# A new order of chunks in the last two layers of a graph network, and a third buffer for gathered rows

## The chip, the cores and the metric

The kernel runs on one core of a Trainium2 chip. The metric is the time of one execution on the device in microseconds (us), as the median of several runs. Engines are named as in the profile: PE is TensorE, PEld its weight loads, DVE VectorE, ACT ScalarE, POOL GpSimd, SP SyncE. POOL issues the gathers (indirect DMAs), SP and ACT the plain DMAs.

## What is computed

Four layers on `x` of 4096 nodes by 256 features, all with the same weighted adjacency matrix `adj` (4096 by 4096, float32, mostly zeros; the first nodes have by far the most neighbours). After each layer the result is added to `x` and normalized by row.

```python
# layer 0: A @ (x * W)
# layer 1: two steps of R @ X and of top-p attention, each with its projections (R = A + I by row sums)
# layer 2
scores = inputs @ H_v
logits = where(adj != 0, adj * scores[None, :], -max)
weights = softmax over a row's neighbours
out = weights @ inputs
# layer 3
neighbor_node_features = adj @ node_features
neighbor_edge_features = einsum('ij,ji->i', adj, edge_features)[:, None]
out = concatenate((node_features, neighbor_node_features, neighbor_edge_features)) @ weight + bias
```

Layer 2 keeps two products of its output: `y3`, through the half of the layer-3 weight that belongs to neighbours, and `t3`, through the half that belongs to the node itself (with the node's own value added). Layer 3 then is `adj @ y3` plus `t3`, an edge term and the bias, and a row normalization.

## The kernel before

Nodes are cut into 32 blocks of 128 rows. A block's sum over neighbours is made in one of two ways:

- **hub blocks**, the first ones (`HUBS = (3, 6)`: three in layer 2, six in layer 3), multiply all 32 column blocks. A hub chunk is four of them: one panel of 256 KB loaded by SP (`loads`, six buffers), and four matmuls against rows that are in SBUF (`X2` in layer 2, `Y3` in layer 3).
- **list blocks**, all others, have a short list of columns found in layer 0 (`CAPS`, 4 to 7 slots of 128 entries). A list chunk is a piece of at most five slots: one packed block loaded by SP (`pc`, six buffers) and, per slot, one gather on POOL of 128 rows (`xg`, 24 buffers) and one matmul.

`product` (L1609) runs a layer: n=0 is layer 2 with rows from `x2d`, n=1 is layer 3 with rows from `y3d`. Layer 2 has 24 hub chunks and 35 list chunks (146 gathers), layer 3 has 48 and 29 (126 gathers). `evenly` (L1604) merges the two sequences by their relative position, so both last to the end. In this one sequence, `fetch` (L1616) issues loads and gathers for the chunk three places ahead (`FETCH = 3`), `weigh` (L1633) prepares the next chunk, and `multiply` (L1637) does the matmuls of the present one. In layer 2 `weigh` is `nbr_weights` (L1589): one ACT exponential per slot, one DVE product per chunk (L1593). Layer 3 has nothing to weigh. PE, ACT, DVE and POOL carry their work in the order that is written out; a queue that stands at a wait holds all behind it. SP is filled by a scheduler.

When a block's sum is complete, its end follows one chunk later: `out_2` (L1669) divides, normalizes on DVE, transposes and projects on PE (L463), and writes `y3d` (ACT queue, L1682) and `t3d` (SP queue, L1685). `out_3` (L1698) adds the bias, the edge term and `t3` (L1700 to L1702, the last reading the sum from PSUM), normalizes and writes the output. `before_3` (L1693) loads a block's `t3` back (`t3r`, seven buffers) with the block's first chunk. A sum in PSUM belongs to one bank: hub blocks use the bank A (`acc_tile("A")`), list blocks alternate between two others. Gathers of layer 3 (POOL) wait until all of `y3d` is written.

The change also touches the first attention step of layer 1, the "narrow" stage. There 32 blocks run through a pipeline whose pieces have planned times (`AT`, L1122). Per block, piece W (L1253) computes the index of five times 128 listed rows, pieces G0 to G4 (`fetch`, L1255) gather these rows on POOL into tiles `g_0`, `g_2` and `g_4` (two buffers each), piece PK (L1270) transposes part of them on PE, and piece PSA (L1313) multiplies them; this frees the tiles for the block after the next.

Of the kernel before, what the change touches and what calls it, by code (L numbers as in the profile page):

```python
# [11 lines left out]
F32 = mybir.dt.float32  # L12
# [6 lines left out]
P = 128  # L19
# [23 lines left out]
NB = 5  # L43
ORDER = (1, 3, 0, 2, 4)

TW = D + DA
# [3 lines left out]
NEW = 7  # L50
HUBS = (3, 6)
FETCH = 3
NM = 4
GUESS = (1.2, -0.129)
SLOPE, AIM, NEAR, MOVE, FEW = 0.07, 16, 32, 1.5, 70
# [12 lines left out]
LC = 512  # L68
# [5 lines left out]
def gnn_kernel(ctx: ExitStack, tc: tile.TileContext, x, pair, panels, W0, W1, W2T, W3T, U1T, U2T,  # L74
# [33 lines left out]
    def bank(shape, name, tag):  # L108
        if name in own_bank:
            tag = name  # L110
        return pools["psum"].tile(shape, F32, name=name, tag=tag, bufs=n_banks.get(tag, 1))
# [20 lines left out]
    for j in range(NT):  # L132
        t = big.tile([P, D + 1], F32, name=f"xw_{j}", tag=f"xa{j}", padded_shape=[P, D + 2])
# [80 lines left out]
    def acc_tile(which):  # L214
        return bank([P, 512], "acc", f"acc{which}")
# [175 lines left out]
    def gather(o, src, idx, c):  # L391
        nc.gpsimd.indirect_dma_start(out=o, out_offset=None, in_=src,  # L392
                                     in_offset=bass.IndirectOffsetOnAxis(ap=idx[:, c], axis=0))
# [160 lines left out]
    def find_0():  # L554
        for b in range(LE, NT):
            e = pools["e"].tile([P, N], F32, name="e")
            for h in range(NT // HB):
                t = e[:, h * HB * P:(h + 1) * HB * P]
                nc.sync.dma_start(t.rearrange("p (c x) -> p c x", x=JC * P),
                                  panels[b, h * HB // JC:(h + 1) * HB // JC].rearrange("c p k i -> p c (k i)"))  # L560
                yield
                nc.vector.tensor_reduce(seen[:, h * HB:(h + 1) * HB, b], t.rearrange("p (t i) -> p t i", i=P), AX.X,
                                        OP.max, apply_absolute_value=True)
# [54 lines left out]
    with tc.manual_schedule(engines=everything):  # L618
        sums_of_edges = edges_0()
        dense = (step for I in range(LE) for step in dense_0(I))  # L620
        find, lists, others = find_0(), list_columns(1, True), None
        left, active, n, heads = list(range(LE, NT)), [], 0, 3
# [17 lines left out]
        lists = others  # L640
# [250 lines left out]
    def cut(a):  # L891
# [3 lines left out]
        u, r = facts[n]["u"][:, I:I + 1], facts[n]["r"][:, I:I + 1]  # L895
        ties = small.tile([P, NM], F32, name="ties")
        nc.vector.tensor_scalar(rest, cand.rearrange("p a b -> p (a b)"), u, None, op0=OP.is_equal)
        nc.vector.tensor_reduce(ties, rest.rearrange("p (a b) -> p a b", a=NM), AX.X, OP.add)
        left = small.tile([P, NM], F32, name="left")
        nc.vector.tensor_tensor_scan(left, ones.to_broadcast([P, NM]), ties, r, op0=OP.mult, op1=OP.subtract)  # L900
        nc.vector.tensor_add(ties, ties, left)
# [3 lines left out]
        nc.vector.tensor_scalar(ties, ties, a["ud"], u, op0=OP.mult, op1=OP.add)  # L905
        m = N // NM
        for g in range(NM):
            eg = e[:, g * m:(g + 1) * m]
# [202 lines left out]
    for k in range(2):  # L1111
        t = const.tile([P, N // P + 1], BF16, name=f"ranks_{k}")
# [17 lines left out]
    def narrow(I):  # L1130


        sp, at_I, a = pools["sp"], slice(I, I + 1), {}
# [120 lines left out]

        def fetch(k):  # L1255
            if k % 2 == 0:
                a["pair", k] = sp.tile([P, 2 if k < NB - 1 else 1, TW], F32, name=f"g_{k}", bufs=2)
            to = a["pair", k - k % 2][:, k % 2, :]
            at_end = k % 2 == 0 and k < NB - 1
            gather(to, tab if at_end else tak, a["idx"], slice(k, k + 1))  # L1260
            a["g", k] = to[:, :D] if at_end else to[:, DA:]
# [109 lines left out]
    at = {}  # L1371
# [19 lines left out]
    def r_stream(blocks):  # L1391
        due, t = [], 0
        for b in blocks:
            if b == DENSE:
                run(lists)
            for _ in r_one(b, lambda f: due.append((t + LATE, f))):
                t += 1
                while due and due[0][0] <= t:
                    due.pop(0)[1]()
                yield  # L1400
        for _, f in due:
            f()

    everything = {getattr(mybir.EngineType, k) for k in ("PE", "Activation", "DVE", "Pool")}
    with tc.manual_schedule(engines=everything):
        r_blocks = list(range(LE, NT)) + list(range(DENSE, LE))
        side = r_stream(r_blocks)
# [37 lines left out]
    def r_dense():  # L1445

        stage = e_tile(2)
        xs = stage[:, :N // 2].rearrange("p (s k i) -> p s k i", s=2, k=JC)
        more = stage[:, N // 2:].rearrange("p (s b k i) -> p s b k i", s=2, b=2, k=JC)
        ps = [acc_tile("A"), acc_tile("R"), bank([P, 512], "acc2", "tp")]  # L1450
        given = {}

        def fetch(c):
            if c < NT // JC:
                pc = pools["gat"].tile([P, PIECE, P], F32, name="pc", bufs=N_PC[0])
                given[c] = [pc[:, :JC], more[:, c % 2, 0], more[:, c % 2, 1]]
                nc.sync.dma_start(xs[:, c % 2], qtab[c * JC * P:(c + 1) * JC * P, :].rearrange("(k p) d -> p k d", p=P))
                for b, t in enumerate(given[c]):
                    nc.sync.dma_start(t, panels[b, c])

        fetch(0)
        for c in range(NT // JC):
            fetch(c + 1)
            for k in range(JC):
                for b in range(DENSE):
                    nc.tensor.matmul(ps[b][:, :D], given[c][b][:, k, :], xs[:, c % 2, k], start=(c + k == 0),
                                     stop=(c * JC + k == NT - 1))
                yield
        for b in range(DENSE):
            new_t(b, ps[b], reload(qpd[b], 0))  # L1470

    none = iter(())
    with tc.manual_schedule(engines=everything):
        rest = r_dense()
# [122 lines left out]
    for I in range(NT):  # L1597
        t = big.tile([P, D + 2], F32, name=f"x2_{I}", tag=f"xa{I}")
# [2 lines left out]
    ends_in = ["x3", 4]  # L1601
    Y3 = [pools["x3"].tile([P, D], F32, name=f"y3_{I}") for I in range(NT)]

    def evenly(a, b):  # L1604

        turns = [((k + 0.5) / len(x), n, x[k]) for n, x in enumerate((a, b)) for k in range(len(x))]
        return [what for _, _, what in sorted(turns, key=lambda t: t[:2])]

    def product(n, src, width, inside, order, weights, end, first=None):  # L1609

        hubs = [(I, c, None) for I in range(HUBS[n]) for c in order]
        lists = [(I, m, ab) for I in range(NT - 1, HUBS[n] - 1, -1) for m, ab in enumerate(pieces(I))]
        chunks = evenly(hubs, lists)
        given, made, ps, going, at, had = {}, {}, {}, [], {}, {}

        def fetch(t):  # L1616
            I, m, ab = chunks[t]
            if first and I not in had:
                had[I] = first(I)
            if ab is None:  # L1620
                pc = pools["loads"].tile([P, JC, P], F32, name="panel", tag="panel")
                nc.sync.dma_start(pc, panels[I, m])
                given[t] = pc, inside[m * JC:(m + 1) * JC]
                return
            pc = pools["gat"].tile([P, PIECE, P], F32, name="pc", bufs=N_PC[0])
            nc.sync.dma_start(pc[:, :ab[1] - ab[0]], packed[I][m])
            xs = []
            for k in range(*ab):
                xs.append(pools["gat"].tile([P, src.shape[1]], F32, name="xg", padded_shape=[P, D + 2]))
                gather(xs[-1], src, idx_x, col(I, k))  # L1630
            given[t] = pc, xs

        def weigh(t):  # L1633
            pc, xs = given.pop(t)
            made[t] = (weights(pc, xs, len(xs)) if weights else pc), xs

        def multiply(t):  # L1637
            I, m, ab = chunks[t]
            if I not in ps:
                ps[I] = (bank([P, 2, LC], "acc", "lg")[:, 0, :] if ab and I % 2 else acc_tile("R" if ab else "A"))  # L1640
                at[I] = 0
            pc, xs = made.pop(t)
            n_all = NT if ab is None else CAPS[I]
            for k, xg in enumerate(xs):
                nc.tensor.matmul(ps[I][:, :width], pc[:, k, :], xg[:, :width], start=(at[I] == 0), stop=(at[I] == n_all - 1))  # L1645
                at[I] += 1
            if at[I] == n_all:
                going.append(end(I, ps[I], had.get(I)))

        with tc.manual_schedule(engines=everything):  # L1650
            for t in range(min(FETCH, len(chunks))):
                fetch(t)
            weigh(0)
            for t in range(len(chunks)):
                if t + FETCH < len(chunks):
                    fetch(t + FETCH)
                if t + 1 < len(chunks):
                    weigh(t + 1)
                before = list(going)
                multiply(t)  # L1660
                for g in before:
                    if next(g, g) is g:
                        going.remove(g)
            while going:
                for g in list(going):
                    if next(g, g) is g:
                        going.remove(g)
# [174 lines left out]
```

## Time and profile before

| | us |
|---|---|
| median of 3 runs (2638.25 to 2649.78) | 2639.12 |
| the profiled execution | 2997.28 |
| its span, first to last instruction | 2995.5 |
| layer 0 (first to last L549 matmul) | 4.4 to 482.6 |
| narrow stage (first to last L1313 matmul) | 585.8 to 1331.0 |
| layer 1, second step (L1086 matmuls) | 1430.2 to 2482.2 |
| layer 2 (list matmuls, L1645) | 2514.5 to 2756.9 |
| layer 3 (hub matmuls, L1645) | 2759.5 to 2983.3 |

| engine | busy us | share of the span |
|---|---|---|
| PE | 2275.7 | 76% |
| DVE | 2073.9 | 69% |
| POOL | 1694.0 | 57% |
| ACT | 1480.6 | 49% |

The profiled execution is one run with the profiler on, and is longer than the median run. A line of the timeline reads: start, length, engine, source line, operation, what it writes and reads, how many, and in brackets how long the engine had been idle before and what ended that. "remote" or "another core or an unknown queue" stands where nothing in the profile accounts for the end of a wait, "issue" where the engine waited for nothing that the profile shows. A float32 matmul leaves two records on PE.

### The profile page before, as it was taken

To read this page: it belongs to the slowest core of one execution; us is meant where nothing else is said; L and a number is where in the kernel's file an instruction comes from. 1 tells how busy PE (TensorE), PEld (TensorE's weight loads), DVE (VectorE), ACT (ScalarE), POOL (GpSimd) and SP (SyncE) were. 2 spreads that over 40 slices of the span, in tenths; PEclk is the share of its full clock that TensorE was granted. 3 is DMA by queue.
4 is the path that set the end of the run, shared out by engine and by line. 5 is a ranking of instruction groups with operands and counts; after the bars stand their busy time and mean duration, and the time that the engine had idled before them with its cause. 6 is when DMAs were issued, how large, how long until landed. Compare 5 with 4: busy or idle time off the path is not lost.

```text
span 2995.5 us, 37683 instructions
## 1 busy us (share of the span) xinstructions
PE 2275.7 (76%) x10680; PEld 1616.2 (54%) x10680; DVE 2073.9 (69%) x6152; ACT 1480.6 (49%) x2413; POOL 1694.0 (57%) x2778
## 2 busy tenths in 40 slices
PE   7887787677666776667988888888878864787587
PEld 5675564344333443435766666666656653555475
DVE  5785455765565665626578999999999991766366
ACT  0000112455454554545678888888899941343000
POOL 1007774444444444444358888888888754662663
PEclk9998898787777877778999999999999987899798
DMA  9978874333333333345531111111111115564574
GB/s 323 336 252 294 252 232 151 101 113 114 98 86 98 91 100 94 93 117 167 176 107 59 54 51 46 56 49 45 60 40 40 49 34 174 174 207 149 168 248 139
DMA packets 261978, 392.17 MB, mean 131 GB/s; under 512 B 41920, under 2 KB 170320, under 8 KB 260992
## 3 DMA queue, kind: packets, MB, share of 16 engines
q1 hardware_dynamic: 160992, 203.82, 21.5%
q0 software_dynamic: 46112, 131.50, 15.3%
q10 hardware_dynamic: 54656, 54.35, 5.3%
q8 instruction: 88, 1.44, 0.2%
q14 instruction: 130, 1.06, 0.1%
HBM read 329.25 MB, written 60.26 MB: 130 GB/s over the span
## 4 chain that ended last, share of the span: by engine, by line
DVE 18%; PE 17%; POOL 6%; issue 6%; ACT 6%; another core or an unknown queue 2%; DMA 0%; ACTq 0%; DVEq 0%; SPq 0%; POOLq 0%
PE acc L1645 5%; PE psa L236 4%; DVE cand L867 3%; PE acc L1086 2%; DVE e L913 2%; DVE tmp L861 2%; POOL xg L392 2%; PE lg L670 2%; DVE e L909 2%; ACT junk L780 2%; PE pt L225 1%; DVE top L844 1%; DVE rest L846 1%; PE po L463 1%
## 5 line engine op out<-in xcount | busy, mean ns | idle before, releaser
L236 PE MATMUL psa<-v,eT 128*128 128x256 f32 x2048 | 508.3, 395 | 74.9 <-ACT eT L227 68.0
L236 PEld LDWEIGHTS psa<-v,eT 128*128 128x128 f32 x2048 | 397.9, 198 | 153.4 <-ACT eT L227 87.4
L549 PE MATMUL acc<-xw,panel 128*128 128x257 f32 x1024 | 258.5, 403 | 35.0 <-DMA panel<-in_panels 22.4
L780 ACT ACTIVATE junk<-e,h 128x4096 bf16<-128x4096 f32 x64 | 237.5, 3711 | 47.3 <-POOL h L760 34.8
L549 PEld LDWEIGHTS acc<-xw,panel 128*128 128x128 f32 x1024 | 200.4, 202 | 92.7 <-issue 34.3
L392 POOL DMA_INDIRECT g<-tab,idx x64 | 63.1, 985 | 312.9 <-PE acc L1313 221.9
L225 PE MATMUL pt<-ident,e 128*128 128x128 f32 x1024 | 157.5, 284 | 101.4 <-DVE e L913 68.9
L786 ACT ACTIVATE junk<-e,h 128x4096 bf16<-128x4096 f32 x62 | 230.8, 3723 | 0.1
L247 ACT COPY xT<-ptx 128x256 f32<-128x256 f32 x96 | 35.7, 372 | 360.3 <-PE ptx L244 181.7
L463 PE MATMUL po<-u,xT 128*128 128x512 f32 x256 | 172.3, 810 | 51.0 <-ACT xT L247 26.2
L225 PEld LDWEIGHTS pt<-ident,e 128*128 128x128 f32 x1024 | 130.3, 147 | 145.4 <-issue 95.8
L867 DVE MAX8 cand<-tmp 128x8 f32<-128x128 f32 x1024 | 203.8, 281 | 1.1
L392 POOL DMA_INDIRECT xg<-qtab,idx_x x146 | 140.1, 959 | 93.6 <-issue 34.9
L227 ACT COPY eT<-pt 128x512 f32<-128x512 f32 x256 | 144.6, 588 | 91.3 <-PE pt L225 90.4
L392 POOL DMA_INDIRECT xg<-x2d,idx_x x146 | 144.3, 988 | 80.4 <-issue 38.7
L392 POOL DMA_INDIRECT pc<-in_pair,idx_a x146 | 149.2, 1022 | 66.3 <-issue 37.9
L392 POOL DMA_INDIRECT xg<-y3d,idx_x x126 | 120.9, 960 | 109.9 <-DMA t3d<-t 43.7
L1158 ACT ACTIVATE e<-lg 128x1024 f32<-128x1024 f32 x128 | 131.0, 1024 | 103.0 <-remote 58.5
L392 POOL DMA_INDIRECT xg<-ttab,idx_x x146 | 144.8, 992 | 60.5 <-issue 33.4
L1166 DVE MAX8 cand<-e 128x8 f32<-128x256 f32 x512 | 176.0, 412 | 3.2 <-ACT e L1158 3.2
L1155 PE MATMUL lg<-kT,qi 64*128 64x512 f32 x512 | 155.9, 684 | 2.9 <-DVE qp L515 2.5
L909 DVE SCALAR_TENSOR_TENSOR e<-e,ties 128x1024 f32<-128x1024 f32 x128 | 156.0, 1281 | 2.9
(347 smaller groups left out, 5674.3 us busy)
## 6 DMA issues: line engine op xcount, KB each, us to landing
panel<-in_panels SPq DMA_DIRECT2D x200, 256.0 KB
e<-in_panels SPq DMA_DIRECT2D x64, 512.0 KB
pc<-pk SPq DMA_DIRECT2D x53, 320.0 KB
e<-in_hubs ACTq DMA_DIRECT2D x6, 2048.0 KB
xg<-ttab SPq DMA_DIRECT2D x96, 128.0 KB
pc<-pk SPq DMA_DIRECT2D x39, 256.0 KB
pc<-in_panels SPq DMA_DIRECT2D x32, 256.0 KB
tab<-xi ACTq DMA_DIRECT2D x33, 160.0 KB
```

Source lines behind the costliest of these rows:

```text
L225: nc.tensor.transpose(pt[:, k, :], e[:, (g * 4 + k) * P:][:, :P], ident)
L236: nc.tensor.matmul(ps[:, :D], eT[g][:, k, :], rhs[j][:, :D], start=(j == 0), stop=stop and j == NT - 1)
L392: nc.gpsimd.indirect_dma_start(out=o, out_offset=None, in_=src, in_offset=bass.IndirectOffsetOnAxis(ap=idx[:, c], axis=0))
L463: nc.tensor.matmul(po.rearrange("p a b -> p (a b)"), xT[:, h, :], u[:, h, :], start=(h == 0), stop=(h == 1))
L549: nc.tensor.matmul(ps[:, :D + 1], a[:, k, :], XW[j][:, :D + 1], start=(j == 0), stop=(j == NT - 1))
L780: nc.scalar.activation(junk_tile(), e, AF.Relu, bias=h, scale=-1.0, accum_out=part)
L786: nc.scalar.activation(junk_tile(), e, AF.Sign, bias=h, scale=-1.0, accum_out=below)
L867: nc.vector.max(cand[:, c * (NS // 2) + g, :], w[:, g * SEG:(g + 1) * SEG])
L909: nc.vector.scalar_tensor_tensor(eg, eg, ties[:, g:g + 1], eg, op0=OP.is_gt, op1=OP.mult)
L1155: nc.tensor.matmul(a["lg", c][:, k, :], a["qi"][r, :], kT[r, c * LC:(c + 1) * LC], start=True, stop=True)
L1166: nc.vector.max(a["cand"][:, b, :], a["e"][:, b * SEG0:(b + 1) * SEG0])
L1645: nc.tensor.matmul(ps[I][:, :width], pc[:, k, :], xg[:, :width], start=(at[I] == 0), stop=(at[I] == n_all - 1))
```

## The change

- `fetch` in the narrow stage gives the tiles `g_` three buffers instead of two.
- `evenly` becomes `in_order`. The first `LEAD` hub chunks (5 in layer 2, 12 in layer 3) stand before everything; the other hub chunks are spread over the first three quarters (`SPREAD`) of the list chunks; the last quarter has lists alone.
- In layer 3 hub blocks are taken by pairs (`side = 2`): each column chunk is done for both blocks in turn. The second block of a pair has its sum in a bank of the tag `tp`.
- `fetch_ahead` counts hubs and lists apart: of each kind, the chunk in hand and three more are fetched.

The sequence of chunks (H hub, L list) of layer 2 before and after, then of layer 3:

```
LHLHLLHLHLLHLHLHLLHLHLLHLHLLHLHLLHLHLLHLHLLHLHLHLLHLHLLHLHL
HHHHHLHLHLHLLHLHLLHLHLHLLHLHLLHLHLHLLHLHLHLLHLHLLHLLLLLLLLL

HLHLHHLHHLHLHHLHHLHLHHLHHLHLHHLHHLHLHHLHHLHLHHLHHLHLHHLHHLHLHHLHHLHLHHLHHLHLH
HHHHHHHHHHHHHLHLHHLHHLHLHHLHHLHLHHLHHLHLHHLHHLHLHHLHHLHLHHLHHLHLHHLHHLLLLLLLL
```

```diff
--- before.py
+++ after.py
@@ -50,6 +50,7 @@
 NEW = 7
 HUBS = (3, 6)
 FETCH = 3
+LEAD, SPREAD = (5, 12), 0.75
 NM = 4
 GUESS = (1.2, -0.129)
 SLOPE, AIM, NEAR, MOVE, FEW = 0.07, 16, 32, 1.5, 70
@@ -1254,7 +1255,7 @@
 
         def fetch(k):
             if k % 2 == 0:
-                a["pair", k] = sp.tile([P, 2 if k < NB - 1 else 1, TW], F32, name=f"g_{k}", bufs=2)
+                a["pair", k] = sp.tile([P, 2 if k < NB - 1 else 1, TW], F32, name=f"g_{k}", bufs=3)
             to = a["pair", k - k % 2][:, k % 2, :]
             at_end = k % 2 == 0 and k < NB - 1
             gather(to, tab if at_end else tak, a["idx"], slice(k, k + 1))
@@ -1601,16 +1602,21 @@
     ends_in = ["x3", 4]
     Y3 = [pools["x3"].tile([P, D], F32, name=f"y3_{I}") for I in range(NT)]
 
-    def evenly(a, b):
-
-        turns = [((k + 0.5) / len(x), n, x[k]) for n, x in enumerate((a, b)) for k in range(len(x))]
-        return [what for _, _, what in sorted(turns, key=lambda t: t[:2])]
+    def in_order(hubs, lists, lead):
+
+        rest = hubs[lead:]
+        turns = [((k + 0.5) / len(rest) * SPREAD, 0, what) for k, what in enumerate(rest)]
+        turns += [((k + 0.5) / len(lists), 1, what) for k, what in enumerate(lists)]
+        return hubs[:lead] + [what for _, _, what in sorted(turns, key=lambda t: t[:2])]
 
     def product(n, src, width, inside, order, weights, end, first=None):
 
-        hubs = [(I, c, None) for I in range(HUBS[n]) for c in order]
+        side = 1 + n
+        hubs = [(I, c, None) for A in range(0, HUBS[n], side) for c in order for I in range(A, A + side)]
         lists = [(I, m, ab) for I in range(NT - 1, HUBS[n] - 1, -1) for m, ab in enumerate(pieces(I))]
-        chunks = evenly(hubs, lists)
+        chunks = in_order(hubs, lists, LEAD[n])
+        turn_of = [[t for t, c in enumerate(chunks) if (c[2] is None) == hub] for hub in (True, False)]
+        fetched, passed = [0, 0], [0, 0]
         given, made, ps, going, at, had = {}, {}, {}, [], {}, {}
 
         def fetch(t):
@@ -1630,6 +1636,12 @@
                 gather(xs[-1], src, idx_x, col(I, k))
             given[t] = pc, xs
 
+        def fetch_ahead():
+            for kind, turns in enumerate(turn_of):
+                while fetched[kind] < min(len(turns), passed[kind] + 1 + FETCH):
+                    fetch(turns[fetched[kind]])
+                    fetched[kind] += 1
+
         def weigh(t):
             pc, xs = given.pop(t)
             made[t] = (weights(pc, xs, len(xs)) if weights else pc), xs
@@ -1637,7 +1649,9 @@
         def multiply(t):
             I, m, ab = chunks[t]
             if I not in ps:
-                ps[I] = (bank([P, 2, LC], "acc", "lg")[:, 0, :] if ab and I % 2 else acc_tile("R" if ab else "A"))
+                ps[I] = (bank([P, 512], "acc", "tp") if ab is None and I % side else
+                         bank([P, 2, LC], "acc", "lg")[:, 0, :] if ab and I % 2 else acc_tile("R" if ab else "A"))
+            if I not in at:
                 at[I] = 0
             pc, xs = made.pop(t)
             n_all = NT if ab is None else CAPS[I]
@@ -1648,16 +1662,15 @@
                 going.append(end(I, ps[I], had.get(I)))
 
         with tc.manual_schedule(engines=everything):
-            for t in range(min(FETCH, len(chunks))):
-                fetch(t)
+            fetch_ahead()
             weigh(0)
             for t in range(len(chunks)):
-                if t + FETCH < len(chunks):
-                    fetch(t + FETCH)
+                fetch_ahead()
                 if t + 1 < len(chunks):
                     weigh(t + 1)
                 before = list(going)
                 multiply(t)
+                passed[chunks[t][2] is not None] += 1
                 for g in before:
                     if next(g, g) is g:
                         going.remove(g)
```

## The prediction

> **What bounds the kernel now.** I read the page first (span, engines, costliest groups), then the waits by stage, then the timelines of the three places that the diff touches. The groups show where GpSimd (POOL), which issues every gather, stands still; the waits table for the narrow stage shows waits that nothing in the profile releases:
>
> ```profile
> L392 POOL DMA_INDIRECT g<-tab,idx x64 | 63.1, 985 | 312.9 <-PE acc L1313 221.9
> ...
> L392 POOL DMA_INDIRECT xg<-y3d,idx_x x126 | 120.9, 960 | 109.9 <-DMA t3d<-t 43.7
> ```
> ```profile
> ACT kT L298 <- remote: 75.5, 19, 10.0
> ...
> ACT e L1158 <- remote: 58.5, 14, 7.5
> ```
>
> The first line invites a third buffer: POOL waits 222 us for the matmul that reads the listed rows of two blocks earlier. The timeline of one period shows what stands behind that wait:
>
> ```profile
> 932.59 0.49 PE L1270 MATMUL pk<-ident,g 128*128 128x128 f32 x3
> ...
> 933.05 2.40 PE L1313 MATMUL acc<-g,wT 128*128 128x256 f32 x10
> ...
> 934.51 0.16 DVE L1253 SCALAR_TENSOR_TENSOR idx<-want,pi 128x5 int32<-128x5 f32 x1
> ...
> 935.42 0.95 POOL L392 DMA_INDIRECT g<-tab,idx  x1 [10.62 <-PE acc L1313]
> ```
>
> The gather starts when the matmul ends (935.45), but its own index is only ready at 934.67. The rows gathered in the period before (911.0 to 918.5) are first read by the transposes at 932.59, 14 us after the last of these gathers was issued.
>
> Second place, the start of layer 2 (start, length, engine, line): ScalarE waits for a list's packed block, then TensorE gets its first matmul.
>
> ```profile
> 2510.40 0.40 ACT L1592 ACTIVATE pe<-pc,xg 128x128 f32<-128x128 f32 x1 [9.14 <-DMA pc<-pk]
> ...
> 2514.50 3.39 PE L1645 MATMUL acc<-xg,pe 128*128 128x257 f32 x8 [20.66 <-DVE pe L1593]
> ```
>
> Third place, layer 3: the last projection of layer 2, the first gather, the first list, two changes of hub block, the last gathers and the last matmuls.
>
> ```profile
> 2765.15 1.98 PE L463 MATMUL po<-wl,xT 128*128 128x512 f32 x4 [0.46 <-ACT xT L247]
> ```
> ```profile
> 2770.32 0.95 POOL L392 DMA_INDIRECT xg<-y3d,idx_x  x1 [43.66 <-DMA t3d<-t]
> ```
> ```profile
> 2772.99 1.22 PE L1645 MATMUL acc<-xg,pc 128*128 128x256 f32 x2 [5.11 <-DMA xg<-y3d,idx_x]
> ...
> 2832.15 3.78 PE L1645 MATMUL acc<-y,panel 128*128 128x256 f32 x8 [9.55 <-DVE y L1701]
> ```
> ```profile
> 2956.54 0.95 POOL L392 DMA_INDIRECT xg<-y3d,idx_x  x1 [0.30 <-issue]
> ...
> 2960.19 2.95 PE L1645 MATMUL acc<-y,panel 128*128 128x256 f32 x8 [4.47 <-DVE y L1702]
> ...
> 2981.84 1.89 PE L1645 MATMUL acc<-y,panel 128*128 128x256 f32 x8
> ```
>
> Gathers that follow without a pause are 1.253 us apart (2770.32, 2771.57, ...), so the 126 of layer 3 need 158 us and the 146 of layer 2 need 183. TensorE's records in a full stretch take 16 in 3.47 us (2838.68 to 2842.13 and others), 0.435 us a matmul of two records; layer 3 has 318 matmuls, 138 us. After its last gather layer 3 still runs 32 us, because hubs are spread to the very end. So layer 3 is bound by gathers plus a tail. In layer 2 TensorE has 242 matmuls (105 us) and, for 32 blocks, 1.72 us of projection and 0.35 of transposes (66 us), 171 in all; VectorE some 179 (32 block ends of 4.3 us, 59 products of 0.69); POOL 183: three engines close together, and 262 us used.
>
> **The Trainium skill.** "Perfetto Trace Analysis", Summary: the profiler window per engine type, says TensorE's reported end is estimated and that a SWDGE (GpSimd-issued) DMA's window leaves out the moving of the data. The trace agrees: ScalarE reads `psq` 2.7 us after its matmuls' recorded end, and a gather's 0.95 us is followed by data 2.65 us after its start (chain of waits). "DMA: Bandwidth & Descriptors", Anatomy of one DMA, fits a SWDGE DMA as 2.0 us plus bytes over 436e3; for 128 KB that is 2.3 us, near the 2.65. "PSUM — Partial Sum Buffer", The four PSUM rules, has one matmul output within one bank, so two open hub sums need two banks: the trace has PE waiting at each change of hub for VectorE to read the only one (9.55, 4.84, 2.97, 4.47 us).
>
> **The profile against the median.** The profiled execution took 2997.28 us (2995.5 of span), the median 2639.12: 358 more. Much of it must be stalls like the "remote" ones and TensorE's crawl at 2789.6 to 2812 (eight hub matmuls at 1.4 us a record, 22 us for 3.5 us of work). They lie in the stages with gathers. I count no gain from removing them, and give the sum for both times.
>
> **The change, part by part.**
> 1. Third buffer of `g_`. It removes a wait on a matmul that ends at most 0.8 us after the index, block for block; the index wait takes its place. If 0.8 us counted in all 32 blocks it would be 25 us, but the transposes come 8.8 to 17.4 us after the last gather's issue in 29 blocks (7.3, 1.3 and 1.1 in three), so: 0. Bounds 0 and 25. What hides it is that slack; at the median's shorter period it would shrink (I guess to some 6 us), still above 0.8. Behind the gather on POOL are packed-block and neighbour gathers; they start up to 0.8 us sooner, then wait for their own eight row buffers. No loss seen.
> 2. Layer 2, five hubs lead. They need layer-2 rows 0 to 19 and panels, both issued by 2498 in the old order. First exponentials can follow the last x2 (2500.66+0.60), four take 1.27, the product 0.69: TensorE starts at about 2503.4 instead of 2514.5. Twenty matmuls of 0.435 = 8.7 us of path work fall into time when TensorE had nothing. The 20 exponentials (6.3 us) are ahead of the first list's on ScalarE, which could not start before 2510.4 anyway. Worth 8.7; bounds 0 (if gathers set the pace at once) and 11.
> 3. Layer 2, remaining 19 hubs over three quarters. POOL in that part has 114 gathers, 143 us; TensorE 114 list and 76 hub matmuls (83) and 27 block ends (56), 139: balanced, and 24 row buffers (30 us) take up unevenness. The nine list pieces at the end, 32 gathers, are gather-paced. One block ends last instead of a list and a hub: before, the last sum (2757.3) to the last projection (2767.1) took 9.8 us; one end alone is 3.9 of VectorE, 0.4 transposes, 0.4 copy, 2.0 projection plus signals, 7.3. Worth 2.5; bounds 0 and 11.
> 4. Layer 3, twelve hubs lead. In the new order 17 of the first 52 hub matmuls stand inside layer 2's tail and 35 (15.2 us) between the last projection and the first list. They fill the 5.1 us wait; 4 stand there now. The second sum of a pair has a bank that no one uses in these layers. Nothing on POOL moves: its first gather still waits for the last y3 write.
> 5. Layer 3, pairs and three quarters. TensorE has 301 matmuls (131 us) after the last projection; POOL needs 3.2 to its start and 158. End: last gather landed (2.65), four matmuls (1.75), one block end (4.4), and the 5.6 us that follow the last VectorE work today: 3.2+158+2.65+1.75+4.4+5.6 = 175.6 us. Two changes of pair replace five of hub; a pair ends with two VectorE chains of 4.4, so about 6 us each, inside TensorE's 30 us of room. Today the same stretch is 2995.5-2767.1 = 228.4. Without the crawl (18.5), with the first hub change at the others' size (5 less) and without seven gaps of about 1 us at single matmuls (7) it is 198. I leave 3 us of POOL waits in the new 175.6: worth 19; bounds 6 (only the tail) and 34 (only the crawl taken out). The first three quarters move some 32 MB (48 panels, 22 list blocks, 95 gathers) in about 135 us, 237 GB/s; windows today reach 297, so I count nothing for it; at the mean of 2812 to 2900, 227 GB/s, it would lose 6.
> 6. Own fetch counts. Up to four hubs and four lists are ahead instead of three chunks. With a pair open, eight `t3r` loads can want seven buffers; SyncE then holds panels and blocks behind that load. Six panels are already in place (10 us of matmuls); I take 0, bounds 0 and 6 lost, twice.
>
> Sum: 0+8.7+2.5+0+19+0 = 30.2, so 2639.1-30.2 = 2609 at the median. For a profile like this one part 5 is worth 228.4-186 (allowing 10 us of POOL waits from a crawl), 42: 2997.3-53 = 2944.
>
> **Rivals.**
> (a) Gathers already set the pace in unprofiled runs. Then TensorE's lead is worth nothing and only tails shrink: 2.5 in layer 2; in layer 3 a list, a hub and two ends (about 13) become a list and one end (6): 9 in all, 2630. For: POOL's 183 is near layer 2's need. Against: POOL waits 37 us there (22.4 for sums, 5.8 for transposes, 8.4 for nothing shown).
> (b) Slower: continuous gathering slows TensorE. The two runs of over 30 gathers without a pause (2504 to 2542, 2770 to 2810) are the two places where TensorE's results stalled, 23.5 and 18.5 us. The change lets POOL run with fewer pauses; 272 gathers are eight such runs. Three more stalls of 21 us: 2609+63 = 2672. From two more on, the kernel is slower. Against: the median says most such stalls belong to the profiled execution.
> (c) The third buffer counts too: 25 more, 2584.
>
> **Chances.** Forecast 0.55 (2592 to 2625), (a) 0.20 (2626 to 2642), (b) 0.15, (c) and layer-2 pacing at its upper bound 0.10 (2570 to 2591). The range from 2580 to 2642 holds the first two and half of (c). A measurement of this kernel tells about 0.5%, 13 us, from no change: faster 0.65, same 0.20, slower 0.15.
>
> **What would show it.** Right: `g` gathers wait for `idx` about as long as now; the first layer-2 matmul within 3 us of 2503; no wait for y3d rows on TensorE; at most two waits for the hub bank; under 12 us from the last gather's issue to the last VectorE work. Wrong: POOL still waiting 20 us or more for `acc` in layer 3; panel waits on TensorE; a shorter narrow stage.

## The result and the profile after

| | median us | runs | ratio to the kernel before |
|---|---|---|---|
| before, runs beside the changed kernel | 2640.37 (2638.25 to 2649.78) | 5 | |
| changed kernel | 2625.37 (2622.47 to 2627.68) | 5 | 0.9926 [0.9908, 0.9944] |
| before, on a chip with a lower granted TensorE clock | 3026.41 (3019.37 to 3038.63) | 11 | |
| changed kernel, on that chip | 3003.13 (2998.51 to 3006.82) | 6 | 0.9914 [0.9894, 0.9934] |

The change is worth 0.74%, 15 us by the two medians and 19.5 (14.8 to 24.3) by the ratio, where 30 were forecast. The runs fall into two groups. In some the kernel before has a mean granted TensorE clock of 0.93 to 0.94 and takes about 2640 us, in others 0.875 to 0.885 and about 3026. In the experiments one chip gave only the first kind and two others only the second; whether the chip itself is the reason, or what else went on at that time, was not tested. "Higher clock" and "lower clock" are names for the two kinds here and not a cause: at every moment the clock in these traces is either 1.00 or 0.50, and the mean tells how long it stood at the half. The profile that the prediction was read from (clock 0.884, 2997.28 us) is of the second kind, the median that it was laid against (2639.12) of the first. So I profiled the kernel before once more, with the higher clock; "before" below is this execution unless the first profile is named.

From the page: the span of before, its slices of TensorE's busy time, and the granted clock.

```profile
span 2645.2 us, 37683 instructions
...
PE   6888689679988998869788888888888875888797
...
PEclk8999889779999999989999999999999997999999
```

The same of the changed kernel:

```profile
span 2625.9 us, 37696 instructions
...
PE   6887789679988988869888888888888877798997
...
PEclk8999899779999989889999999999999998899997
```

The clock row is the quickest way to see which kind of execution one has. The first profile's row reads 9998898787777877778999..., with 7 and 8 in the narrow stage.

Next the groups that show GpSimd's waits: operation, count | busy us, mean ns | idle us before it, and what ended it. Before:

```profile
L392 POOL DMA_INDIRECT xg<-x2d,idx_x x146 | 146.4, 1003 | 46.9 <-issue 24.7 <-PE acc L1645 9.4 <-DMA xg<-x2d,idx_x 5.5
L392 POOL DMA_INDIRECT xg<-y3d,idx_x x126 | 121.7, 966 | 72.6 <-DMA t3d<-t 34.5 <-issue 18.0 <-PE acc L1645 13.1
L392 POOL DMA_INDIRECT g<-tab,idx x64 | 64.2, 1003 | 86.0 <-issue 33.2 <-PE acc L1313 28.2 <-DVE idx L1253 13.3
```

After:

```profile
L393 POOL DMA_INDIRECT xg<-x2d,idx_x x146 | 147.1, 1007 | 46.7 <-issue 22.0 <-PE acc L1659 10.4 <-DMA xg<-x2d,idx_x 7.9
L393 POOL DMA_INDIRECT xg<-y3d,idx_x x126 | 121.5, 964 | 59.2 <-DMA t3d<-t 21.1 <-issue 17.7 <-PE acc L1659 14.3
L393 POOL DMA_INDIRECT g<-tab,idx x64 | 63.6, 993 | 90.0 <-issue 41.5 <-DVE idx L1254 39.1 <-PE cs L1204 4.3
```

Three readings. Layer 2's gathers wait as little before as after (46.9 and 46.7 us, nearly all of it the 0.3 us between two issues). Layer 3's only real wait is the one before its first gather, 34.5 us and then 21.1. And the third buffer turned 28.2 us of waiting for `acc` into more waiting for `idx`. The 222 us of waiting for `acc` in the first profile are not there at the higher clock.

The stretches of both layers, cut at the first and last gather of each (stretch, its length, busy us and records of PE, PEld, DVE, ACT and POOL, clock, DMA share, GB/s). Before:

```profile
2239.80:2429.20 189.40, 158.39 (x588) 110.80 (x588) 137.31 (x471) 85.31 (x274) 145.21 (x146) 0.92 0.74 225
2429.20:2464.90 35.70, 27.78 (x102) 18.39 (x102) 21.64 (x78) 10.28 (x32) 1.20 (x2) 0.95 0.38 115
2464.90:2623.70 158.80, 140.11 (x584) 111.93 (x585) 112.89 (x407) 0.00 (x0) 120.73 (x125) 0.96 0.80 257
2623.70:2645.20 21.50, 9.87 (x46) 8.36 (x44) 10.76 (x40) 0.00 (x0) 0.95 (x1) 0.83 0.11 34
```

After:

```profile
2242.70:2433.10 190.40, 169.87 (x650) 120.92 (x651) 145.30 (x495) 90.20 (x292) 146.14 (x146) 0.96 0.75 230
2433.10:2455.10 22.00, 19.57 (x77) 13.35 (x76) 12.50 (x47) 4.63 (x14) 0.92 (x1) 1.00 0.54 175
2455.10:2613.80 158.70, 142.63 (x589) 112.83 (x587) 121.10 (x441) 0.00 (x0) 120.53 (x126) 0.93 0.78 253
2613.80:2625.90 12.10, 3.71 (x7) 1.50 (x6) 3.05 (x12) 0.00 (x0) 0.95 (x1) 0.50 0.12 39
```

The two stretches with gathers keep their length: 189.4 and 190.4, 158.8 and 158.7. In layer 3 the first to the last gather is 125 times 1.27 us in both kernels: no gather waits longer than the 0.3 us that lie between any two issues. In layer 2 TensorE does 11.5 us more beside the same gathers. What shrinks is what comes after the last gather: 35.7 to 22.0 and 21.5 to 12.1, 23.1 us in sum. Both layers together go from 405.4 to 383.2 us; the stages ahead of them ended 2.9 us later in this execution, which leaves the 19.3 us between the spans.

The places that the prediction showed, in the changed kernel: the head of layer 2,

```profile
2241.99 4.78 ACT L1593 ACTIVATE pe<-panel,x 128x128 f32<-128x128 f32 x16 [2.49 <-DMA x2d<-x]
...
2244.04 10.97 PE L1659 MATMUL acc<-x,pe 128*128 128x257 f32 x40 [11.96 <-DVE pe L1594]
```

the change of layer,

```profile
2450.34 1.88 PE L464 MATMUL po<-wl,xT 128*128 128x512 f32 x4
2452.06 15.27 PE L1659 MATMUL acc<-y,panel 128*128 128x256 f32 x70
...
2455.14 0.95 POOL L393 DMA_INDIRECT xg<-y3d,idx_x  x1 [21.12 <-DMA t3d<-t]
```

and the end (last gather, its matmul, the last sum's first and last VectorE operation):

```profile
2613.80 0.95 POOL L393 DMA_INDIRECT xg<-y3d,idx_x  x1 [0.30 <-issue]
...
2616.63 1.22 PE L1659 MATMUL acc<-xg,pc 128*128 128x256 f32 x2 [0.16 <-DMA xg<-y3d,idx_x]
2617.89 0.42 DVE L1715 TENSOR_TENSOR y<-y,acc 128x256 f32<-128x256 f32 x1 [5.21 <-PE acc L1659]
...
2620.91 0.41 DVE L278 TENSOR_SCALAR o<-y,mv,rs 128x256 f32<-128x256 f32 x1
```

In before, the same places read:

```profile
2249.48 3.79 PE L1645 MATMUL acc<-xg,pe 128*128 128x257 f32 x8 [20.48 <-DVE pe L1593]
...
2459.69 1.98 PE L463 MATMUL po<-wl,xT 128*128 128x512 f32 x4 [0.46 <-ACT xT L247]
2464.88 0.95 POOL L392 DMA_INDIRECT xg<-y3d,idx_x  x1 [34.51 <-DMA t3d<-t]
2467.57 1.22 PE L1645 MATMUL acc<-xg,pc 128*128 128x256 f32 x2 [5.15 <-DMA xg<-y3d,idx_x]
...
2623.73 0.95 POOL L392 DMA_INDIRECT xg<-y3d,idx_x  x1 [0.30 <-PE acc L1645]
...
2631.68 1.89 PE L1645 MATMUL acc<-y,panel 128*128 128x256 f32 x8
...
2639.30 0.41 DVE L277 TENSOR_SCALAR o<-y,mv,rs 128x256 f32<-128x256 f32 x1
```

Measured from the first gather of layer 2, TensorE's first matmul came 9.7 us after it and now 1.3. From there to the end of the last projection it took TensorE 212.2 us and now 208.2, although 17 matmuls of layer 3 stand in it where 4 stood. So the gain of layer 2 can be read in two ways. Measured along its gathers, whose stretch did not change, all of it lies behind the last one. Measured along TensorE, which had 58 records of the layer left when that gather started, 8.4 of the 12.4 us up to the last projection are its earlier start. That gathers run without a pause shows that nothing holds them; it does not show that the other engines wait for them. The 5.15 us at the start of layer 3 are filled with hub matmuls. From the last gather's start to the last VectorE operation it was 15.6 us, with the hub matmuls at 2631.68 in it; it is 7.1, with one matmul and one block end.

### The profile page after: what moved, and what is told of

It is laid out like the page before. It is cut to its first block, busy times and chain, and to the rows that moved or that the text cites. A ratio compares the mean times of both kernels' runs of the same rounds, so it can differ in the third digit from the quotient of the medians.

```text
span 2625.9 us, 37696 instructions
## 1 busy us (share of the span) xinstructions
PE 2197.5 (84%) x10680; PEld 1572.6 (60%) x10680; DVE 2064.5 (79%) x6152; ACT 1478.7 (56%) x2413; POOL 1704.6 (65%) x2778
## 4 chain that ended last, share of the span: by engine, by line
DVE 22%; PE 18%; POOL 7%; ACT 5%; issue 4%; DMA 2%; SPq 0%; POOLq 0%; DVEq 0%; ACTq 0%
PE psa L237 5%; PE acc L1659 5%; DVE cand L868 4%; DVE tmp L862 3%; PE acc L1087 2%; DVE e L914 2%; DVE top L845 2%; PE lg L671 2%; DVE rest L847 2%; ACT junk L781 2%; PE po L464 1%; POOL xg L393 1%; PE pt L226 1%; DVE e L910 1%; POOL shift L1015 1%
## 5 line engine op out<-in xcount | busy, mean ns | idle before, releaser
L237 PE MATMUL psa<-v,eT 128*128 128x256 f32 x2048 | 515.7, 400 | 81.6 <-ACT eT L228 81.6
L393 POOL DMA_INDIRECT xg<-x2d,idx_x x146 | 147.1, 1007 | 46.7 <-issue 22.0
L1197 ACT ACTIVATE marks<-e,mid 128x1024 bf16<-128x1024 f32 x128 | 140.2, 1144 | 48.9 <-DVE mid L1193 40.8
L393 POOL DMA_INDIRECT xg<-y3d,idx_x x126 | 121.5, 964 | 59.2 <-DMA t3d<-t 21.1
L464 PE MATMUL po<-u,xT 128*128 128x512 f32 x256 | 138.6, 669 | 20.3 <-DVE qp L516 19.8
L742 ACT ACTIVATE e<-lg 128x1024 f32<-128x1024 f32 x120 | 123.5, 1029 | 52.5 <-PE lg L671 52.5
```

What stands on the lines that cost most here:

```text
L237: nc.tensor.matmul(ps[:, :D], eT[g][:, k, :], rhs[j][:, :D], start=(j == 0), stop=stop and j == NT - 1)
L464: nc.tensor.matmul(po.rearrange("p a b -> p (a b)"), xT[:, h, :], u[:, h, :], start=(h == 0), stop=(h == 1))
```

## The experiments

Theory T, formed on the profile after: gathers pace both layers without a pause, and only what is left behind the last gather of a layer counts. Its first rival, L, is the prediction's own reason: TensorE sets the pace, so its head start counts. The first four kernels ran at the higher clock, beside 32 runs of before (2643.96 us median, 2635.19 to 2651.35), the other eight at the lower clock.

**The kernel before, profiled again.** No edit.

> The kernel before, unchanged, for a second profile. If the 358 us by which its first profiled execution exceeded the median belong to that execution alone, the span is 2635 to 2645 and the narrow stage takes some 500 us (as in the changed kernel's profile, 576 to 1067) instead of 745; layer 2 and layer 3 together then take about 15 us more than the 383 us (2243 to 2626) of the changed kernel. If profiling this kernel always costs that much, the span is again near 2990.

2647.0 us, span 2645.2, so profiling alone does not cost the 358 us. It gave the profile read above: 490.8 us from layer 2's first gather to the end in the first profile were 405.4 here, and the narrow stage (first to last matmul of the listed rows) 487.6 instead of 745.2. The two layers took 22.2 us more than in the changed kernel, where 15 were expected.

**The third buffer alone.** On the kernel before:

```diff
-                a["pair", k] = sp.tile([P, 2 if k < NB - 1 else 1, TW], F32, name=f"g_{k}", bufs=2)
+                a["pair", k] = sp.tile([P, 2 if k < NB - 1 else 1, TW], F32, name=f"g_{k}", bufs=3)
```

> The kernel before with three buffers for g_ and nothing else. My theory (the index wait takes the place of the buffer wait): 0 us, within 3. Rival (the wait counts at the median's shorter period, and is part of the 15 us): 5 to 15 us faster.

2645.82 us (14 runs), ratio 1.0006 [0.9993, 1.0018]: nothing. Its group of listed-row gathers, which with two buffers had 28.2 us of `acc` and 13.3 of `idx`:

```profile
L392 POOL DMA_INDIRECT g<-tab,idx x64 | 63.2, 987 | 92.8 <-issue 40.7 <-DVE idx L1253 39.5 <-PE cs L1203 4.9
```

The index took over the wait. POOL waits as long as before, 92.8 us against 86.0.

**One layer alone**, each on the kernel before (third buffer left out): layer 2 in the new order with own counts, layer 3 as before; then the reverse.

```diff
     product(0, x2d, D + 1, X2, panels_of, nbr_weights, end_2)
-    product(1, y3d, D, Y3, panels_of[:1:-1] + panels_of[:2], None, out_3, before_3)
+    product_old(1, y3d, D, Y3, panels_of[:1:-1] + panels_of[:2], None, out_3, before_3)
```

> The new order and fetch counts in layer 2 alone (5 hubs lead, three quarters); layer 3 with the old order, g_ with two buffers. Theory A (prediction's shares, 11 of 30, at half size): 5 us faster. Theory B (gathers already set layer 3's pace before, so layer 3 gained only its tail): 9 to 11 us faster here.

2633.59 us (9 runs), 0.9963 [0.9949, 0.9977], 9.8 us (6.1 to 13.5). This is theory B's figure, twice theory A's.

```diff
-    product(0, x2d, D + 1, X2, panels_of, nbr_weights, end_2)
+    product_old(0, x2d, D + 1, X2, panels_of, nbr_weights, end_2)
     product(1, y3d, D, Y3, panels_of[:1:-1] + panels_of[:2], None, out_3, before_3)
```

> The new order, pairs and fetch counts in layer 3 alone; layer 2 with the old order, g_ with two buffers. Theory A: 10 us faster. Theory B: about 5 us faster, from the tail alone. If the hub leads of layer 3 only help where layer 2's end leaves TensorE idle, this and the layer-2 run sum to less than 15.

2633.77 us (16 runs), 0.9965 [0.9951, 0.9979], 9.2 us (5.6 to 13.0). Here theory A's 10 came and theory B's 5 did not. The two add up to 1 minus 0.0072, the whole change's 0.0074. With `layer2_only` layer 3's part is that of before (179.8 us from its first gather to the end, before 180.3); with `layer3_only` it is the new one (170.1, changed kernel 170.8). Layer 3's share is then 9.5 us by the stretches and 9.2 by the timed runs, and lies wholly behind the last gather. In layer 2 the pause goes from 35.7 to 21.7 us with `layer2_only`, more than the timed 9.8; but single executions of the old layer 2 differ (32.9 to 36.7 us in the three at this clock), so a pause is not good to better than some 3 us. The two runs show what each layer is worth. They do not show which of its parts does it: lead, spread, own counts and, in layer 3, pairs came together.

**Single parts undone, first four.** Each is the changed kernel with its own leads and shares (by layer, so `in_order` takes the layer's `spread`); here the second of the four, with layer 2 spread to the end:

```diff
-LEAD, SPREAD = (5, 12), 0.75
+LEAD, SPREAD = (5, 12), (1.0, 0.75)
...
-        chunks = in_order(hubs, lists, LEAD[n])
+        chunks = in_order(hubs, lists, LEAD[n], SPREAD[n])
```

The others have `(0, 12), (0.75, 0.75)` (`l2_no_lead`), `(5, 0), (0.75, 0.75)` (`l3_no_lead`) and `(5, 12), (0.75, 1.0)` (`l3_spread_to_end`).

> The changed kernel with no hub chunks ahead in layer 2 (24 hubs over three quarters of the lists); layer 3 as changed. Theory T (gathers pace the layer without a pause, so only what is left after the last gather counts): nothing is lost or at most 2 us, 2625 to 2627 us, ratio to the kernel before 0.993, and GpSimd's pause between the layers stays near 21 us. Theory L (the head start that the prediction priced at 8.7 us is what counts): 2634 us, ratio 0.996, and a pause near 30 us.

> The changed kernel with layer 2's remaining 19 hubs spread over all of its lists, five still ahead; layer 3 as changed. Theory T: most of layer 2's 9.8 us are given back, 2632 to 2636 us, ratio 0.996, and GpSimd's pause between the layers goes from 21 back to 30 us or more. Theory L (three quarters are worth the 2.5 us of the prediction): 2628 us, ratio 0.994, and a pause of 23 to 24 us.

> The changed kernel with no hub chunks ahead in layer 3 (48 hubs in pairs over three quarters of the lists); layer 2 as changed. Theory T: the lead fills time in which TensorE waited, and its 12 hubs fit into TensorE's room beside 158 us of gathers: 2625 to 2628 us, ratio 0.993 to 0.994, and the stretch from the first gather of y3d rows to the end stays within 2 us of 170.8. Theory L (without the lead TensorE falls behind the gathers): 5.2 us lost for 12 matmuls of 0.435, 2631 us, ratio 0.995.

> The changed kernel with layer 3's remaining hubs, still in pairs and with twelve ahead, spread over all of its lists; layer 2 as changed. Theory T: the 9.2 us of layer 3 are given back, or more, since now two hub sums end last instead of one: 2634 to 2640 us, ratio 0.996 to 0.9985, and 20 us or more from the last gather's end to the end. Theory L (the head start counts more than the tail): 2627 to 2630 us, ratio 0.994, with 13 to 16 us after the last gather.

These runs had the lower clock, so the expectations in us do not apply; the ratios do. The changed kernel itself was not run beside them; in the next group it has 0.9914. Beside 12 runs of before (3027.68 us): no lead in layer 2 0.9918 [0.9893, 0.9943], layer 2 spread to the end 0.9936 [0.9916, 0.9955], no lead in layer 3 0.9932 [0.9915, 0.9949], layer 3 spread to the end 0.9925 [0.9899, 0.9951]. The intervals overlap one another and all keep most of the gain. Theory T was right on the two leads (nothing lost) and missed the two spreads (0.996 and more); theory L was right on the two spreads (0.994) and missed the two leads (0.995 to 0.996).

**The changed kernel at the lower clock, and parts undone in both layers at once.** `after_again` has no edit, `no_lead` has `(0, 0), 0.75`, and the two others are

```diff
-LEAD, SPREAD = (5, 12), 0.75
+LEAD, SPREAD = (5, 12), 1.0
```

(`spread1`) and

```diff
-        side = 1 + n
+        side = 1
```

(`no_pairs`).

> The changed kernel unchanged, on the chip of the other three runs. Both theories: the ratio 0.9926 of the first measurement, within 0.002. If the execution has the lower granted clock of the first profile of the kernel before (0.88 instead of 0.94), theory C (TensorE's lower clock makes it the bound of layers 2 and 3, and the changed order helps there too) expects 3003 us, 0.992, and gaps in the gathers of layer 3; the prediction's 53 us would be 0.982.

> The changed kernel without hub chunks ahead in either layer; pairs, three quarters, own counts and third buffer stay. Theory T (gathers pace both layers, only what is left after the last gather counts): at most 3 us more than the changed kernel, ratio to it up to 1.001. Theory L (the head start counts: 8.7 us in layer 2 and 5.2 in layer 3): 14 us more, 1.0053.

> The changed kernel with the remaining hubs spread over all the lists in both layers; leads, pairs, own counts and third buffer stay. Theory T: 15 to 20 us more than the changed kernel, 1.006 to 1.0075 to it, so within 0.002 of the kernel before; with the higher clock GpSimd's pause between the layers is 30 us or more and 20 us pass from layer 3's last gather to the end. Theory L: 2.5 us more in layer 2 and some 3 in layer 3, 1.002.

> The changed kernel with layer 3's hub blocks one after the other instead of in pairs (side 1); leads, three quarters, own counts and third buffer stay. Theory T: with gathers as the pace five waits for the hub bank of about 3 us each fit into TensorE's room, so 0 to 1 us more than the changed kernel. Rival (TensorE has no room left in the three quarters): three more bank waits of 3 to 4.5 us, 10 us more, 1.004.

Again the lower clock, beside 11 runs of before (3026.41 us):

| | median us | ratio to before |
|---|---|---|
| changed kernel (`after_again`) | 3003.13 | 0.9914 [0.9894, 0.9934] |
| `no_lead` | 3004.37 | 0.9915 [0.9892, 0.9937] |
| `spread1` | 3003.15 | 0.9922 [0.9896, 0.9948] |
| `no_pairs` | 3007.32 | 0.9937 [0.9914, 0.9960] |

`after_again` came as theory C said: 3003 us, and pauses in the gathers (those longer than 0.35 us sum to 47 us in layer 2 and 29 in layer 3). The 0.982 of the prediction's 53 us did not come. `no_lead` lost 1.2 us, as theory T had it and not the 14 of theory L. `no_pairs` lost 4.2, between the 0 to 1 of theory T and the 10 of its rival; its interval tells it from neither. `spread1` should have lost 15 to 20 us by theory T, and lost 0.02 by the medians and 2.4 by the ratios. The stretches suggest why. `after_again`, cut as above (gathers of layer 2, pause, layer 3 to the end):

```profile
2534.30:2762.00 227.70, 174.10 (x607) 119.57 (x608) 136.31 (x460) 84.05 (x274) 143.32 (x146) 0.87 0.63 186
2762.00:2794.00 32.00, 30.84 (x120) 20.88 (x119) 21.95 (x82) 9.59 (x30) 0.91 (x1) 1.00 0.58 166
2794.00:3005.00 211.00, 152.09 (x595) 122.15 (x593) 124.71 (x453) 0.00 (x0) 120.89 (x126) 0.86 0.61 193
```

`spread1`:

```profile
2521.70:2737.50 215.80, 163.56 (x561) 113.07 (x562) 133.37 (x453) 79.92 (x259) 142.34 (x145) 0.87 0.65 191
2737.50:2781.70 44.20, 37.62 (x149) 26.39 (x148) 25.07 (x88) 14.32 (x45) 0.96 (x2) 1.00 0.42 128
...
2781.70:2999.20 217.50, 156.50 (x611) 124.36 (x610) 124.71 (x453) 0.00 (x0) 121.40 (x126) 0.86 0.60 190
```

The pause between the layers did grow as theory T said, by 12.2 us. But the gathers before it took 11.9 us less. In these executions they wait for TensorE's sums (20.8 of the 47 us in `after_again`, 9.2 of 34 in `spread1`), and in `spread1` TensorE had not yet done the hub matmuls that now stand behind the last gather. The two together are 259.7 and 260.0. A matmul moved from one to the other changed a wait, not the time. So theory T does not hold where gathers wait; whether its forecasts for single parts hold where they do not was not tried. The whole table, one profiled execution each, in us:

| clock | kernel | layer 2, first to last gather | pause | layer 3, first gather to end | sum |
|---|---|---|---|---|---|
| higher | before | 189.4 | 35.7 | 180.3 | 405.4 |
| | third buffer alone | 187.8 | 36.7 | 180.8 | 405.3 |
| | layer 2 alone | 188.9 | 21.7 | 179.8 | 390.4 |
| | layer 3 alone | 188.6 | 32.9 | 170.1 | 391.5 |
| | changed | 190.4 | 22.1 | 170.8 | 383.2 |
| lower | before (first profile) | 221.1 | 44.6 | 225.2 | 490.8 |
| | changed | 227.7 | 32.1 | 211.0 | 470.8 |
| | no lead in layer 2 | 229.8 | 31.9 | 211.2 | 472.9 |
| | no lead in layer 3 | 228.7 | 33.0 | 210.7 | 472.4 |
| | no lead in either | 227.1 | 33.4 | 213.6 | 474.2 |
| | layer 2 spread to the end | 216.7 | 47.0 | 211.5 | 475.1 |
| | layer 3 spread to the end | 224.6 | 32.9 | 216.7 | 474.1 |
| | both spread to the end | 215.9 | 44.2 | 217.5 | 477.5 |
| | no pairs | 226.8 | 31.5 | 214.2 | 472.5 |

At the lower clock no single part holds the 20 us. By these single executions both spreads are 6.7 us of it, both leads 3.4, the pairs 1.7; the timed runs show none of them apart from zero. Whether leads and spread stand in for one another, or the own counts matter there, was not tried. At the higher clock the lead and the three quarters were not taken apart: no run with one of them undone had it. No version is shown to beat the changed kernel.

## Why the prediction was right, and where it was not

The time (2625.4) lies inside the range, 16 us above the forecast and at the edge of the forecast's own band, and nearer to rival (a). The range (2580 to 2642) was wide enough to take in no change at all (2639), so that it was met says little. The sign held, and somewhat over half of the size; the step that carried most of the sum was twice too large. By its steps:

1. **Third buffer, 0.** Right. The index wait took the place of the buffer wait as worked out from the first profile, and `third_buffer_only` measured 1.0006. Rival (c) fell with it: 25 us would have been 0.9905.
2. **Layer 2, five hubs lead, 8.7.** The head start came: 8.4 us sooner relative to the first gather (9.7 to 1.3), 20 matmuls in one piece of 10.97 us. It was forecast 2.6 us earlier still (2503.4 against the first gather at 2504.65 in the first profile): ScalarE's first exponential did not follow the last `x2` at once but stood idle for 2.49 us, put down to the `x2d` store. What it is worth by itself was not settled: measured along TensorE it would be the 8.4 us, but at the lower clock leaving the lead out lost nothing that was clear of noise.
3. **Layer 2, rest over three quarters, 2.5.** The reason given did not come. From the last sum to the last projection 9.8 us were to become 7.3; they are 9.9 before (2451.8 to 2461.7) and 10.2 after (2442.1 to 2452.2), because the ends of two list blocks still follow each other on VectorE. What shrank is the store of layer-2 matmuls behind the start of the last gather: 24 hub and 34 list records before, 0 and 18 after, 40 records or 20 matmuls of 0.435 us, 8.7 us. How much of that the lead did and how much the spread is open. Steps 2 and 3 together, 11.2 forecast, measured 9.8 (6.1 to 13.5). The sum was right; how it divides is not shown.
4. **Layer 3, twelve hubs lead, 0.** Right: the 5.15 us wait is gone, and POOL's first gather still follows the last write.
5. **Layer 3, pairs and three quarters, 19.** This step failed, in one term. The new stretch from the last projection to the end was forecast at 175.6, or 178.6 with the 3 us left for POOL waits, which did not come, and measured 173.7 (2452.2 to 2625.9). The old one, "Without the crawl (18.5), with the first hub change at the others' size (5 less) and without seven gaps of about 1 us at single matmuls (7) it is 198", measured 183.5 (2461.7 to 2645.2). So stripping the stalls from the first profile left 14.5 us too much in it, and 19 should have been 9.8, near its lower bound 6, "only the tail". Two things were left in. The crawl was read as eight matmuls of work; the timeline has eight records there, four matmuls, and from the last record at the full rate (2789.2) to the next one (2817.9) 28.7 us pass for 20 records, 4.3 us of work: some 24 us lost, not 18.5. And in the first profile 64 hub and 36 list records stand behind the last gather, where before at the higher clock has 30 and 14: 56 records of 0.217 us, 12 us of tail that the stripping did not touch. The two overlap in part; their shares of the 14.5 are estimates.
6. **Own counts, 0.** Nothing shows against it: layer 3 has one wait of over 1 us for VectorE (1.98), none for panels, and gathers without a pause. It was not tried alone.

The crawl in the first profile, from the last eight records at the full rate to the list after it (eight hub records in all):

```profile
2787.72 1.89 PE L1645 MATMUL acc<-y,panel 128*128 128x256 f32 x8
2790.66 0.38 PE L1645 MATMUL acc<-y,panel 128*128 128x256 f32 x1 [1.05 <-issue]
...
2809.55 0.59 PE L1645 MATMUL acc<-y,panel 128*128 128x256 f32 x1 [1.53 <-issue]
2811.65 0.59 PE L1645 MATMUL acc<-xg,pc 128*128 128x256 f32 x1 [1.51 <-issue]
```

Two other readings of the first profile were wrong. The 2.7 us from the matmuls of `psq` to ScalarE's reading were laid to TensorE's estimated end; in before that time is 0.46 us in the median of the 32 blocks' copies (4.3 in the first profile), so most of it belongs to that execution. And the wait of 4.84 us counted as one for the hub bank has "issue" behind it in the timeline, not VectorE. The 2.3 us worked out there for a gather is an estimate; the sum used the 2.65 of the trace.

The figure for "a profile like this one", 53 us less, fell too: at the lower clock the change brought 23.3 us (3026.41 less 3003.13). Its part 5 let the crawl go; the crawl stayed. TensorE in layer 3 of `after_again`:

```profile
2810.46 0.38 PE L1659 MATMUL acc<-xg,pc 128*128 128x256 f32 x1 [0.37 <-issue]
2811.85 0.38 PE L1659 MATMUL acc<-xg,pc 128*128 128x256 f32 x1 [1.01 <-issue]
2813.26 0.59 PE L1659 MATMUL acc<-xg,pc 128*128 128x256 f32 x1 [1.04 <-issue]
2816.05 0.59 PE L1659 MATMUL acc<-xg,pc 128*128 128x256 f32 x1 [2.20 <-issue]
2818.86 0.58 PE L1659 MATMUL acc<-xg,pc 128*128 128x256 f32 x1 [2.22 <-issue]
2821.65 0.59 PE L1659 MATMUL acc<-xg,pc 128*128 128x256 f32 x1 [2.21 <-issue]
```

**Rivals.** (a), 0.20, named the pacing rightly for layer 3 at the higher clock: GpSimd never waited there in before either, and in the changed kernel TensorE waits for rows. For layer 2 it is open whether TensorE's lead is worth nothing, as (a) says. Its price was too small, 9 us, since it counted in layer 2 a last list and hub instead of the 29 matmuls that stood behind the last gather. The result lies between it (2630) and the forecast (2609). (b), slower, did not come: at the higher clock the changed kernel issues 126 gathers in a row, TensorE is busy 142.6 us of 158.7 beside them, and no crawl shows; the same holds for the kernel before. The two stalls that spoke for it belong to the lower clock. A crawl some 15 to 20 us after layer 3's first gather is in the profiles of both kernels there, so that gathers take part in it is not ruled out.

**What was to show it.** The waits of the listed-row gathers for `idx` were to stay as long as now: they grew by the length of the `acc` wait. The first matmul came 2.6 us later than its mark, within the 3 us allowed. No wait for y3d rows was to be seen on TensorE: there is none at layer 3's start, but later there are 14, of 1.7 us at most and 11.4 in sum, TensorE having caught up with the gathers. This mark was missed. Of layer 3's waits for VectorE one is longer than 1 us (1.98, before a list's matmul). Last gather to the start of the last VectorE operation: 7.1 us, under 12.

## What to carry to other kernels

Before a profile is stripped of its stalls to make it fit a shorter median, take it again, or compare its time and its mean granted clock with those of the timed runs: gathers that wait for TensorE in one kind of execution run without a pause in the other, and what is moved there has another price. Where a queue of gathers runs without a pause and keeps its length, count the work that stands behind its last one, engine by engine. But such a queue may only be running ahead: look as well whether the others wait for it, and if a part of the change is to be priced, undo that part alone, in the kind of execution that counts. A shorter pause is only a gain if the stretch before it did not grow by the same amount.

## What the runs showed of the hardware

The kernel before takes 14.5% longer in one kind of execution than in the other (3026.41 over 2643.96 us). In its two profiles the granted clock stands at 0.50 for 699 of 2995 us and for 341 of 2645, and at 1.00 otherwise; that is all that the means of 0.884 and 0.936 say. The stages do not suffer alike. The first 580 us have a mean of 0.89 in both, and TensorE is busy for 451.3 and 454.9 us. From 580 to 1067 us the mean is 0.79 against 0.97, and TensorE does 1962 records where it did 2920.

In the crawl above, a record comes every 2.80 us, where a full stretch has 0.217. The records themselves last 0.59 us; between them TensorE waits for nothing that the profile shows. From 2815 to 2830 us the granted clock is 0.50. The Trainium skill, "TensorE: Matmul & The Clock Gate", section What's actually happening, lists two states of that clock, half and full, and the trace agrees: where records of `after_again` follow without a gap they are 0.43 us apart at 0.50 (2828.5 to 2832.4). So the half explains a factor of 2, not of 13. The rest was there before the clock fell: the two records at 2810.46 and 2811.85 are 1.4 us apart, and from 2809.5 to 2812.5 the clock was 1.00. In the first profile too the crawl begins at 2789.5 and the half clock at 2793.8. The low clock did not start these crawls; what did was not found. Waits that nothing in the profile releases go with the same executions: in the narrow stage of `l2_no_lead` stands

```profile
ACT kT L299 <- remote: 88.5, 20, 11.5
```

and in the same stage of before at the higher clock the list of waits has none of that kind.

GpSimd issued 126 gathers of 128 KB, one every 1.25 to 1.27 us with 0.3 us between them, at some 255 GB/s with the panels beside them. TensorE's records kept 0.218 us beside the first of them (70 records in 15.27 us).
